# Two banded-mixing layers: the band product with the right projection stationary, in blocks of 128 rows by 128 columns

## The chip, the core and the metric

The kernel runs on one core of a Trainium2 chip, as one launch, in 32-bit floating point throughout. The metric is the device time of that launch in microseconds (us). The kernel before takes 4958.63 us, the median of three runs (4953.22 to 4959.0).

Five engines of the core work side by side, each through its own instructions in order: TensorE (PE; its weight loads are shown apart as PEld), VectorE (DVE), ScalarE (ACT), GpSimd (POOL), and SyncE (SP), which here only issues DMAs. Matrix products land in PSUM, eight banks of 512 floats per partition; everything else is held in SBUF, 128 partitions wide. A matrix product keeps one operand in the array (the stationary operand, put there by a weight load) and streams the other past it (the moving operand).

## The reference

The input `x` is 512 by 512 positions with 64 channels. Two layers are applied, each as `x = x + conv(group_norm(x))`. Cut to what matters, a layer is:

```python
xn = layer_norm(group_norm(x))                 # group norm: 32 groups of 2 channels, over all positions
left  = (xn @ Wl) * mask * sigmoid(xn @ Wlg)   # 64 -> 128 channels
right = (xn @ Wr) * mask * sigmoid(xn @ Wrg)
gate  = sigmoid(xn @ Wog)
# band: for every output row i, offsets d in -4..4
out[i, j, h] = sum_d left[i + d, i, h] * right[i + d, j, h]
out = layer_norm(out) * gate                   # over the 128 channels
y = out @ Wo                                   # 128 -> 64 channels, then x + y
```

Only nine entries per column of `left` are needed, those within four rows of the diagonal. For each hidden channel `h` the band is a matrix product over rows: a banded matrix made of `left`, times `right`. The second layer's group norm needs the channel sums and the channel square sums of the first layer's whole result, so the second layer begins only when the first has ended.

## The kernel before

**Blocks and chunks.** A row block is 64 rows, and consecutive blocks overlap by 8 rows, so a block gives 56 result rows (60 at the two edges); nine blocks cover 512 rows (`row_blocks`, line 67). The 128 partitions hold the same 64 rows twice, once for column `j` and once for column `j + 256`. A chunk is one row block by 128 such column pairs, so a layer has 18 chunks. A chunk has 16 units of 8 column pairs. A layer's loop (`layer`, line 704) runs over steps `t`, one input unit per step, and everything else is hung on that count.

**What a step does.** The order within a step is written out by hand (lines 765 to 847), and every call goes through a wrapper (lines 365 to 378) that keeps each engine's queue in that order:

- `load` (390) fetches a unit of `x`; `affine` (426) applies the group norm, two POOL operations per unit; `inner_stats` and `inner_norm` (431, 435) are the layer norm, four DVE statistics and two POOL operations.
- `transposed` and `kept` (441, 460) turn the unit by TensorE and copy it to `zT` with ScalarE; `kept` also stores it to a DRAM buffer `later`.
- `right` (487), twice per step: four products with a 64x128 piece of `zT` stationary, a sigmoid on ScalarE, and a DVE product into the big SBUF tile `RO`.
- `left` (497) runs five times at the start of a layer (steps 3, 5, 7, 9, 11). It computes the entries near the diagonal and writes them by small DMAs into a DRAM buffer `left_of`, which was filled with zeros first. `take_left` (527) reads it back as the banded matrix `A`.
- `mix` (539) is the band product, for 8 channels at a time, 16 calls per chunk. `A` (64 x 64, columns 16 floats apart in memory) is stationary and `RO` (64 x 128) moves; the two partition halves work in opposite corners of the array. The result goes back over `RO`, half by ScalarE and half by DVE.
- `out_stats` and `solve` (571, 577) give the mean and the inverse deviation of the result; `solve` runs every fourth step, some four operations on DVE and some twelve on POOL, for the input and the output norm together.
- `norm` (610): eight ScalarE operations per output unit. `recall` and `gates` (618, 622): the unit's `zT` is read back from `later`, and its gate is computed by two products of 448 moving columns per unit. `turned` (641): sixteen transposes, then two DVE operations that multiply by the gate into `ZH`. `end` (673): sixteen products with `Wo`, added to the residual `XR`, which POOL has biased (`biased`, 667), and stored.
- `sums` (692), in the first layer only: eight products per unit gather the channel sums and square sums in one PSUM bank. For the sums, a column of ones stands on either side of each piece of `XR`, so its rows are 130 floats long.

An output unit trails its input unit by 30 steps (`LAG`, line 707).

**Buffers.** PSUM holds two double banks (`ps2`, for `right`, `transposed` and `mix`), three single banks in the first layer and four in the second, and one bank for `sums`.

**Start.** 300 us go by with the group statistics of `x`, the weights, and the zero fill of `left_of`. The scratch pool of the set-up is freed then, and the tiles that take its place (`RO`, `XR`, `ZH`) wait for the zero fill that reads it.

## Time and profile before

| what | value |
|---|---|
| median of three runs | 4958.63 us |
| span of the profiled execution | 4957.7 us |
| PE busy | 4186.4 us (84%) |
| DVE, ACT, POOL busy | 3836.3, 3645.2, 3826.5 us |
| DMA engines' mean busy share, steady part | 0.72 |
| mean granted TensorE clock | 0.940 |

The profile lists, for each engine, how long its instructions were busy, and groups equal instructions with their count, busy time and mean duration in ns. Three further views are used below: busy time by stretches of the span, the waits (who waited for whom, in total, times, and the longest), and the timeline (instructions in order of time, equal neighbours merged). A `DMA_DIRECT2D` on `SPq` is the issue of a DMA on SyncE's queue, not its transfer. Nearly all code stands under L373, the wrapper's line, so groups are told apart by tile names.

The first output of layer one is biased at 529.9 us and the last at 2622.7 us; in layer two these are 2888.6 and 4949.1 us. In between, a chunk takes 119 us.

### The profile page before, as it was taken

The numbers are of one execution on the slowest core, as the hardware profiler recorded it, in microseconds if no ns is written. First come the engines' busy times: TensorE is split into PE (matmuls) and PEld (weight loads), VectorE is DVE, ScalarE is ACT, GpSimd is POOL, SyncE is SP. The second block draws the span as 40 slices with busy tenths as digits, with TensorE's granted clock in tenths as the row PEclk, the third lists the DMA queues.
The fourth block names the chain that finished last, engine by engine and source line by source line (L and its number), as shares of the span: only waits on it lengthen the run. The fifth ranks groups of instructions, "written<-read, shape, count | busy, mean of one in ns | idle before, by whom it ended". The sixth has DMA issues, their size and how long they took to land. (4 is left out here: it accounts for less than half of the span.)

```text
span 4957.7 us, 173298 instructions
## 1 busy us (share of the span) xinstructions
PE 4186.4 (84%) x67090; PEld 3543.6 (71%) x67090; DVE 3836.3 (77%) x9635; ACT 3645.2 (74%) x8156; POOL 3826.5 (77%) x4739
## 2 busy tenths in 40 slices
PE   1036899999999999999974689999999999999998
PEld 0025788888888888888763577777777777777775
DVE  6855788888888888888766578888888888888876
ACT  0013788888888888888872378888888888888888
POOL 0037888888888888888534788888888998889853
PEclk6558999999999999999996899999999999999999
DMA  7844677777777777777653467777777777777765
GB/s 305 338 156 130 182 203 207 204 207 204 204 203 204 205 206 206 202 207 210 187 143 88 129 181 205 202 207 205 203 206 202 205 206 205 208 207 209 209 184 152
DMA packets 905343, 982.32 MB, mean 198 GB/s; under 512 B 114210, under 2 KB 641608, under 8 KB 900168
## 3 DMA queue, kind: packets, MB, share of 16 engines
q1 hardware_dynamic: 899840, 969.73, 66.9%
q8 instruction: 531, 8.70, 0.8%
q14 instruction: 292, 2.39, 0.2%
q10 hardware_dynamic: 4680, 1.50, 0.1%
HBM read 658.42 MB, written 312.46 MB: 196 GB/s over the span
## 5 line engine op out<-in xcount | busy, mean ns | idle before, releaser
L373 ACT ACTIVATE on<-RO,nm,rs 128x128 f32<-128x128 f32 x4608 | 1872.5, 496 | 130.1 <-POOL nm L373 110.3
L373 PE MATMUL banks<-pack,zT 64*128 64x256 f32 x9360 | 1325.0, 405 | 148.6 <-DVE RO L373 67.8
L373 PEld LDWEIGHTS banks<-pack,zT 64*128 64x128 f32 x9360 | 886.7, 194 | 517.6 <-DVE RO L373 220.1
L373 PE MATMUL banks<-RO,A 64*64 64x128 f32 x18432 | 1154.3, 277 | 12.7 <-ACT zT L373 12.7
L373 DVE TENSOR_TENSOR RO<-banks,sg 128x512 f32<-128x512 f32 x1152 | 789.9, 686 | 421.1 <-ACT sg L373 402.9
L373 PEld LDWEIGHTS banks<-RO,A 64*64 64x64 f32 x18432 | 1082.3, 183 | 38.6 <-ACT zT L373 15.2
L373 ACT ACTIVATE sg<-banks 128x512 f32<-128x512 f32 (+1 forms) x1188 | 695.0, 587 | 372.5 <-PE banks L373 288.6
L373 DVE BATCH_NORM_STATS2 sto<-RO 128x6 f32<-128x256 f32 x2304 | 842.8, 413 | 1.2
L373 DVE SCALAR_TENSOR_TENSOR ZH<-bank,pack,gate 128x448 f32<-128x448 f32 (+1 forms) x1152 | 738.4, 683 | 71.5 <-ACT gate L373 46.9
L373 DVE COPY RO<-banks 128x512 f32<-128x512 f32 x576 | 396.3, 691 | 487.6 <-ACT RO L373 487.0
L373 POOL TENSOR_TENSOR z<-z,gb 128x512 f32<-128x512 f32 x536 | 687.1, 1282 | 42.0
L373 PE MATMUL bank<-pack,ZH 128*64 128x64 f32 x18432 | 682.8, 229 | 6.1 <-ACT gate L373 5.6
L373 POOL TENSOR_TENSOR z<-z,ga 128x512 f32<-128x512 f32 x536 | 687.8, 1283 | 0.1
L373 POOL TENSOR_TENSOR z<-z,rs 128x512 f32<-128x512 f32 x586 | 618.0, 1055 | 46.0
L373 PEld LDWEIGHTS bank<-pack,ZH 128*64 128x64 f32 x18432 | 602.1, 141 | 48.2 <-ACT gate L373 9.6
L373 POOL TENSOR_TENSOR z<-z,sti 128x512 f32<-128x512 f32 x586 | 627.2, 1070 | 0.0
L373 ACT ACTIVATE gate<-bank 128x448 f32<-128x448 f32 (+1 forms) x1152 | 565.9, 543 | 81.1 <-PE bank L373 66.9
L373 PEld LDWEIGHTS bank<-ident,on 64*128 64x128 f32 x9216 | 409.7, 140 | 260.5 <-ACT gate L373 145.3
L373 PE MATMUL bank<-ident,on 64*128 64x64 f32 x9216 | 450.2, 227 | 137.9 <-ACT gate L373 107.3
L373 PE MATMUL bank<-zg,pack 64*128 64x448 f32 (+1 forms) x2304 | 559.5, 558 | 2.2 <-DMA zg<-later 1.5
L373 POOL TENSOR_TENSOR XR<-XR,pack 120x512 f32<-120x512 f32 (+1 forms) x352 | 418.4, 1190 | 160.6 <-DMA XR<-in_x_dram 58.9
L373 ACT COPY RO<-banks 128x512 f32<-128x512 f32 x576 | 333.5, 583 | 234.1 <-PE banks L373 234.0
(145 smaller groups left out, 3683.3 us busy)
## 6 DMA issues: line engine op xcount, KB each, us to landing
later<-zT SPq DMA_DIRECT2D x576, 256.0 KB
A<-left_of SPq DMA_DIRECT2D x576, 256.0 KB
zg<-later SPq DMA_DIRECT2D x576, 256.0 KB
z<-in_x_dram SPq DMA_DIRECT2D x576, 128.0 KB
z<-mid_x SPq DMA_DIRECT2D x576, 128.0 KB
gn_x<-in_x_dram SPq DMA_DIRECT2D x16, 4096.0 KB
XR<-in_x_dram SPq DMA_DIRECT2D x448, 112.0 KB
mid_x<-XR SPq DMA_DIRECT2D x448, 112.0 KB
```

Of the source, the lines that this page charges most:

```text
L373: return lambda *a, **k: tc.keep_in_program_order(f(*a, **k))
```

## The change

A block is now 128 rows, with 120 new rows per block, and a chunk is 128 rows by 128 columns; the last 32 rows of all four column quarters together form one tail chunk. A layer has 4 x 4 + 1 = 17 chunks of 16 input units.

In `mix`, a 64 x 128 piece of `RO` is stationary (columns 2 floats apart) and 64 or 68 columns of `A` move. The result has the 128 columns `j` on the partitions and the rows `i` along the free axis. The halves overlap by 8 rows, which are added by a DVE operation of their own. Each of the 512 x 512 output positions is then normed, gated and projected once: an output unit is 8 rows (or 4, `ni = 1`) by 128 columns, and there are 260 per layer, 8 of them of 4 rows.

Moved and altered with it:

- Input units are 32 rows by 4 x 8 columns, loaded by one DMA. `zT` is a tile of four units. `right` runs four steps later (`LATE`) and takes as stationary operand the same column of all four units, 16 floats apart.
- `later` is laid out by chunk. `recall` reads four runs of 512 bytes per partition where one of 2 KB was read. `gates` becomes eight products of 128 columns.
- `turned` writes its transposes into PSUM with the innermost step 64 floats.
- `left` writes into a free part of `RO` and sends runs of nine floats to DRAM.
- `XR` is contiguous, one DMA each way. The mask is a scalar per partition, so `solve` uses one small operation per column quarter.
- `sums` keeps the square sums; the channel sums come from the accumulating output of the DVE operation in `turned`, added up per chunk.
- The `XR` and `ZH` clearing, the `fewer` constant and its DMAs go.

The core of the diff:

```diff
-JW = 16
+JW = 24
+LATE = 4
+STEP = P - 2 * WIN
+AW = S + 3 * WIN
-HA = 16
-NA = 3
+HA = 8
+NA = 4
@@ load
-            for e, j in enumerate((u.j, LH + u.j)):
-                en.sync.dma_start(u.z[e * S : (e + 1) * S], src[rows, j : j + JU, :])
+            en.sync.dma_start(
+                u.z.rearrange("p j c -> p (j c)"),
+                strided(
+                    src, (i * L + j + 32 * u.s) * D, (L * D, 32), (JU * D, 4), (1, JU * D)
+                ),
+            )
@@ right
+        t = zT[u.n].rearrange("c r (i k g) -> c k g (r i)", k=4, g=4)
+        pr = projected(lambda part, k: t[part, k, u.g], q, w["right"])
@@ left
+                    en.sync.dma_start(
+                        strided(
+                            left_of, ((row + r) * H + t) * AW + a + r,
+                            (R4 * H * AW + R4, nq), (2 * AW, H // 2), (1, NEAR),
+                        ),
+                        side[q0 : q0 + nq, :, t, NEAR * r : NEAR * (r + 1)],
+                    )
@@ mix
-                        ph[part, hh, :], lhsT=A[part, :, h0 % HA + hh],
-                        rhs=R[part, (h0 + hh) // 2, :, hh % 2],
+                        o, lhsT=RO[part, (h1 + h) // 2, c.place : c.place + JC, h % 2], rhs=rhs,
...
+            en.scalar.copy(o[:, :, :m0], x)
+            en.vector.tensor_copy(o[:, :, m0:], y[:, :, v:])
+            if v:
+                o = o[:, :, m0 - v : m0]
+                todo.append((o, o, y[:, :, :v], ALU.add))
@@ norm
-        for j in range(JU):
+        for j in range(R4 * o.ni):
@@ recall
-        en.sync.dma_start(o.t, later[o.at])
+        o.t = t[:, : 256 * o.ni].rearrange("c (s x) -> c s x", s=SUB)
+        en.sync.dma_start(o.t, later[o.chunk.c][:, :, o.i4 * S : (o.i4 + o.ni) * S])
@@ gates
+        for k in range(4):
+            for e, pg in enumerate(pgs):
+                en.tensor.matmul(
+                    pg.rearrange("h (k y s g) -> h k s y g", k=4, s=SUB, g=4)[:, k],
+                    lhsT=w["gate"][part],
+                    rhs=o.t[part].rearrange("c s (y k g) -> c k s y g", k=4, g=4)[:, k],
@@ turned
+                v = pt.rearrange("h (r y s) -> h y s r", r=JU, s=JU)
+                en.tensor.transpose(v[:, i], o.on[part, i, :], ident[part, part])
...
+            more = {"accum_out": acc_to(n)} if acc_to else {}
@@ start
-        z = left_of.rearrange("b (p n) -> (b p) n", n=S * (S + 2 * WIN) // 2)
-        for n in range(0, z.shape[0], P):
-            en.sync.dma_start(z[n : n + P], nothing[: min(P, z.shape[0] - n)])
+        for b in range(n_blocks):
+            for i in range(2):
+                en.sync.dma_start(
+                    left_of[b][:, i * H * AW // 2 : (i + 1) * H * AW // 2], nothing
+                )
```

## Prediction

> **What bounds the kernel now.** I read the busy time by stretches first, one stretch in the steady part of each layer.

> ```profile
> core 0: us, PE busy (x) PEld busy (x) DVE busy (x) ACT busy (x) POOL busy (x), PEclk, DMA share, GB/s
> 900.00:1500.00 600.00, 574.85 (x9991) 502.67 (x9992) 487.70 (x1226) 504.06 (x1127) 534.46 (x642) 0.99 0.72 205
> 3000.00:3600.00 600.00, 551.38 (x8681) 466.47 (x8679) 492.25 (x1224) 502.75 (x1122) 532.92 (x645) 0.98 0.72 204
> ```

> TensorE is busy 96% and 92% of the time, GpSimd 89% in both. A chunk takes 119.3 us in layer one and 118.8 in layer two, although layer two lacks `sums`. What two stretches with different TensorE work and one pace share is GpSimd: 534.5 and 532.9 us. So I ask what it waits for (waits in 3000 to 4200 us; columns: total, times, longest).

> ```profile
> DVE RO L373 <- ACT RO L373: 112.6, 130, 2.0
> PEld banks L373 <- DVE RO L373: 80.6, 140, 1.7
> POOL rsqrt L373 <- DVE rs L373: 61.3, 40, 3.6
> PEld banks L373 <- POOL z L373: 36.7, 36, 1.1
> POOL XR L373 <- DMA XR<-mid_x: 4.4, 6, 1.5
> ```

> GpSimd waits almost only at `solve`, 61 us in 1200 or 6.1 us per chunk. With 106 busy (533 / 600 x 119) that leaves 7 us per chunk, some 80 ns ahead of each instruction, which I count as issue. GpSimd thus has 6 us per chunk to give, and TensorE 5 in layer one and 10 in layer two. Both are near the pace.

> The groups of instructions by shape (count, busy us, mean ns) give the prices:

> ```profile
> L373 PEld LDWEIGHTS banks<-RO,A 64*64 64x64 f32 x18432 | 1082.3, 183 | 38.6 <-ACT zT L373 15.2
> L373 PEld LDWEIGHTS bank<-pack,ZH 128*64 128x64 f32 x18432 | 602.1, 141 | 48.2 <-ACT gate L373 9.6 <-DVE ZH L373 0.6
> L373 PEld LDWEIGHTS bank<-zg,pack 64*128 64x128 f32 x2304 | 225.2, 190 | 34.3 <-DVE ZH L373 3.3 <-DVE RO L373 1.7
> L373 POOL TENSOR_TENSOR XR<-XR,pack 120x512 f32<-120x512 f32 x224 | 266.8, 1191 | 7.1 <-DMA XR<-mid_x 5.7 <-DVE sto L373 1.0 <-DVE RO L373 0.4
> ```

> A weight load of 64 contiguous columns has 141 ns, one of 128 has 190, and the 64 columns of `A`, 16 floats apart, have 183: a wide step makes the load slower. The timeline of one step gives rates:

> ```profile
> 1203.52 0.92 PE L373 MATMUL bank<-zg,pack 64*128 64x448 f32 x4
> 1204.27 1.03 PE L373 MATMUL banks<-pack,zT 64*128 64x256 f32 x8
> 1205.13 0.69 PE L373 MATMUL bank<-ident,on 64*128 64x64 f32 x16
> 1207.65 3.94 PE L373 MATMUL banks<-RO,A 64*64 64x128 f32 x64
> ```

> From start to the next group's start, `gates` takes 0.75 us and `turned` 0.58 (62 ns per pair of halves). Two `mix` calls run to 1211.52 us, 3.87 us or 121 ns per pair. Each fp32 product is two such instructions.

> [...]

> **The change part by part.** Sums are against the profiled span, 4957.7 us, 1 us under the median.

> *Chunks.* 17 for 18: one chunk less per layer, -119 us each, if the pace holds.

> *GpSimd.* Units keep their four operations. Per chunk of 15 output units one `XR` operation goes, -1.2 us, and the mask's small operations add about 1. It stays at 113 us plus up to 6 of waiting.

> *Mix on TensorE.* As many instructions per chunk; 64 columns move instead of 128, but 128 are loaded instead of 64. Loads run under the products before them[...]. I take no change; nothing is won here.

> *Gates.* 8 pairs of 128 columns, taken at the present `mix` rate less its slack, 115 ns: 0.92 us for 0.75. Per chunk 15 x 0.92 - 16 x 0.75 = +1.8.

> *Right.* Its loads step 64 bytes[...]: +2.4 per chunk.

> *Turned.* Sixteen transposes per unit[...]. Below: free [...]; above: doubled, 62 to 124 ns per pair, 0.5 us per unit. I take half, 0.25 x 15 = +3.8 per chunk.

> *One output unit less per chunk* on TensorE: 0.58 + 0.98 (`end`) + 0.57 (`sums`) = -2.1, in layer two -1.6.

> *TensorE's sum per chunk.* Layer one 574.85 / 5.03 = 114.3 + 1.8 + 2.4 + 3.8 - 2.1 = 120.2; with 3 of its 5 us of idle time, 123. Layer two 109.6 + 6.4 = 116; with 2 idle, 118. So TensorE sets the pace in layer one, and stands level with GpSimd (113 to 119) in layer two. Against 119: 16 x 4 - 119 = -55, and 16 x -1 - 119 = -135.

> *DVE and ScalarE.* ScalarE's norms fall from 4608 to 4096, one unit's eight or 3 us per chunk. DVE: the copy in `mix` is an eighth shorter and a small add follows (about 0.2 us), `ZH` is 512 wide instead of 448, and layer one adds two accumulator reads per unit (0.06 to 0.16 us each, its shortest clearing and its shortest tensor operation here). Saved statistics balance it. DVE has 21 us per chunk free; were that gone, the add would cost 3 us per chunk. The four 124-row chunks of a layer split each `mix` in two: within the idle I kept.

> *DMA.* `XR` moves in runs of 2 KB instead of 512 bytes, `zg` the other way; `A` grows from 256 KB x 2 to 304 KB x 2 per 16 channels. The share stays near 0.72. SyncE issues about 6 instead of 10 per step. Hidden; without cover a late `A` would stop TensorE.

> *Left.* 96 DMAs per layer instead of 108, but up to 1024 runs of 36 bytes where there were 128 of 64 to 256. SyncE's timeline, and all DMA in 0.3 us around the first of the 8 KB transfers:

> ```profile
> 352.65 12.65 SPq L373 DMA_DIRECT2D left_of<-sg x27
> ...
> DMA packets 144, 0.01 MB, mean 28 GB/s; under 512 B 144, under 2 KB 144, under 8 KB 144
> ```

> The 144 fall into 28 of that view's 40 slices, 0.21 us or 1.5 ns each. The new DMAs have 853 runs on average: 1.3 us each (estimate), 125 us for 96, where issue alone now takes 12.65 / 27 = 0.47 each, some 50 us. From step 3 to step 16, where `A` is wanted behind them, it is then 125 + 35 for SyncE's other DMAs = 160, for 115 now (324 to 439 us): +45. Then 17 steps to the first output, for 14 now, at 6 us: +18. On the other side `sg` no longer waits for these DMAs (67 us now, both layers), and `zT` has eight steps for its stores. I take +45 per layer, between -25 (issue binds) and +190 (twice the price). Queued behind them on SyncE: `z` loads, seven steps ahead, then `A`, then all of `mix`.

> *Start.* The zero fill grows from 21.2 to 24.9 MB, +10 us at the 385 GB/s that the stretch 240 to 280 us shows. But GpSimd and DVE no longer stand 47 us before `XR` and `ZH` clearing that waits for it; their first units run under it, some -20. Together -10. Channel sums at the layer's end: about nil.

> *Sum.* -55 - 135 + 90 - 10 = -110: a span of 4848, rounded to 4845 as a median.

> **Rivals.**

> - *The waits go and `left` hides.* With TensorE at 119 and 113 per chunk and no longer fill: -119 - 215 - 10, about 4615. For it: ScalarE and SyncE are relieved. Against: TensorE's sums.
> - *The scattered transposes double.* TensorE 124 and 120, pace 127 and 122: +9 - 71 + 90 - 10 = +18, 4975. [...]
> - *Slower: the stationary side costs by its step.* Place: `mix`, 256 pairs per chunk. [...] It decides from about 135 ns per pair: each ns costs 256 x 16 x 2 = 8.2 us, and 110 / 8.2 = 13. For it: `A`'s 183 ns. Against: [...] loads for two halves side by side in `right` today.
> - *Slower: the small runs cost double.* 2.6 us per DMA: +125 per layer, 5095. [...] Against: today's 64-byte runs are cheap.
> - *The change does not do what it says:* 17 chunks and 4096 norms follow from the diff, so only their worth is open.

> **How the numbers follow.** Forecast 0.45 (own range 4740 to 4940), faster still 0.08, doubled transposes 0.20, stationary loads 0.12, small runs 0.12, rest 0.03. 0.2% is 10 us, about what a measurement of this kernel can tell from no change. Faster: 0.42 + 0.08 + 0.05 of the doubled case and rest = 0.55; same 0.05; slower 0.40. The range 4700 to 5110 leaves out the stationary loads and most of the fastest case.

> **What would show it.** Chunks 123 and 118 us apart in the `XR` operations of GpSimd; `mix` at 115 to 125 ns per pair; `turned` 0.6 to 1.1 us; first output of layer one near 560 us. It is wrong if `mix` gets cheaper (then GpSimd alone sets 113 to 119), if loads of `RO` show over 200 ns, or if the `left` DMAs end after 520 us in layer one.

## The result, and the profile after

| | before | after |
|---|---|---|
| median | 4957.11 us (4 runs, 4953.22 to 4959.0) | 5757.2 us (4 runs, 5751.47 to 5773.5) |
| ratio, 95% interval | | 1.1616 [1.1596, 1.1637] |
| span of the profiled execution | 4957.7 us | 5759.5 us |
| first `XR` bias operation on GpSimd, layer one | 529.9 us | 667.2 us |
| from there to the layer's last one | 2092.7 us | 2343.6 us |
| from there to layer two's first | 265.9 us | 418.0 us |
| from there to layer two's last | 2060.5 us | 2321.4 us |

The change is 16% slower where 2% faster was forecast, outside the range too. The four lower rows, read from the two traces, split the 802 us between their spans: 137 and 152 in the fill of the two layers (the time before a layer's first output), 251 and 261 in their steady parts, although a chunk less is worked off in each.

Busy time by stretches, steady part of each layer:

```profile
core 0: us, PE busy (x) PEld busy (x) DVE busy (x) ACT busy (x) POOL busy (x), PEclk, DMA share, GB/s
1500.00:2100.00 600.00, 532.82 (x8938) 506.33 (x8932) 412.82 (x1185) 414.90 (x909) 437.80 (x535) 0.93 0.63 180
4200.00:4800.00 600.00, 515.25 (x7988) 483.42 (x7986) 422.26 (x1083) 424.12 (x935) 460.35 (x557) 0.92 0.65 185
```

Nothing is full any more. In layer one TensorE falls from 96% to 89%, GpSimd from 89% to 73%, and the TensorE clock from 0.99 to 0.93. An engine that is busy for less of a longer time is not the bound; something makes them all wait. The waits in 4200 to 5400 us of the kernel after:

```profile
DVE RO L394 <- ACT sg L394: 238.8, 175, 3.5
ACT sg L394 <- PE banks L394: 189.6, 126, 3.8
PE banks L394 <- DVE RO L394: 145.3, 117, 3.6
POOL XR L394 <- DMA XR<-mid_x: 100.3, 24, 7.4
```

Read from the third line: TensorE waits 117 times for a VectorE copy into `RO`, and from that ScalarE waits for TensorE's projections, and VectorE for ScalarE's sigmoids. The groups by shape show no price that rose enough to explain it (the first line is of the kernel before):

```profile
L373 PEld LDWEIGHTS banks<-pack,zT 64*128 64x128 f32 x9360 | 886.7, 194 | 517.6 <-DVE RO L373 220.1
L394 PEld LDWEIGHTS banks<-pack,zT 64*128 64x128 f32 x8704 | 1164.8, 308 | 729.0 <-DVE RO L394 306.2
L394 PEld LDWEIGHTS banks<-A,RO 64*128 64x128 f32 x17408 | 1109.9, 201 | 104.1 <-ACT RO L394 42.3 <-issue 22.8 <-ACT zT L394 17.1
L394 POOL TENSOR_TENSOR XR<-XR,pack 128x512 f32<-128x512 f32 x504 | 550.0, 1092 | 630.6 <-DMA XR<-mid_x 317.0 <-DMA XR<-in_x_dram 255.5 <-PE bank L394 41.2
L394 DVE DVE_READ_ACCUMULATOR ZH<-bank,pack,gate 128x1 f32 x520 | 43.1, 83 | 0.0
```

The loads of `right`, whose columns now lie 64 bytes apart, went from 194 to 308 ns. Most of that is hidden under the products: in the kernel with both edits of the mixes (below), the two `right` calls of a step take 2.03 us to the next group's start where they took 1.83 before, 3.2 us per chunk. The accumulating output shows as a second instruction (`DVE_READ_ACCUMULATOR`) of 83 ns, where the prediction had 60 to 160.

Then the timeline of one step with two `mix` calls (start, duration, engine, and in brackets the idle time before):

```profile
1500.41 3.98 PE L394 MATMUL banks<-A,RO 64*128 64x64 f32 x64
...
1500.94 3.21 ACT L394 ACTIVATE on<-RO,nm,rs 128x128 f32<-128x128 f32 x8 [1.37 <-DVE ZH L394]
...
1504.06 1.04 ACT L394 COPY RO<-banks 128x512 f32<-128x512 f32 x2
...
1504.65 1.16 DVE L394 COPY RO<-banks 128x448 f32<-128x448 f32 x2 [2.36 <-ACT RO L394]
...
1505.73 0.34 DVE L394 TENSOR_TENSOR RO<-RO,banks 128x64 f32<-128x64 f32 x2
...
1506.08 2.02 PE L394 MATMUL banks<-pack,zT 64*128 64x256 f32 x8 [1.69 <-DVE RO L394]
```

Here the loss can be seen whole. The first call is through at 1502.5 us, but its pair of banks is free only at 1505.9: ScalarE is at its eight norms until 1504.1, VectorE waits for ScalarE's copy, and the overlap add of the first call comes after the copies of both (the loop over `both`, lines 941 to 945). Both double pairs are then held, the next `right` finds none, and TensorE stands for 1.69 us. The `right` that follows takes 2.02 us, where the same eight instructions took 1.03 to 1.13 before: it runs at half clock, which the trace shows granted from 1506.40 to 1509.82 us. In the kernel before, the same step had just enough room: VectorE's copy of the first call ended at 1211.33 us, 0.2 us before the second call was through, and `right` followed without a gap:

```profile
1210.65 0.68 DVE L373 COPY RO<-banks 128x512 f32<-128x512 f32 x1
...
1211.52 1.14 PE L373 MATMUL banks<-pack,zT 64*128 64x256 f32 x8
```

From the start of one `end` on TensorE to the next (layer one), a step without `mix` takes 5.7 us in both kernels, and one with a single `mix` 7.2. A step with two took 9.0 us and now takes 10.9 to 13.5, 12.4 most often. Six steps of a chunk are such. From the first output of a chunk to that of the next it is some 140 us in layer one and 133 to 143 in layer two, and 151 to 165 us for the first four chunks of a layer. Those have an output unit more, and beside the outputs of the first three run the split `mix` calls of the next 124-row chunk.

The fill is the other part. SyncE's timeline and all DMA from 330 to 500 us:

```profile
323.25 38.67 SPq L394 DMA_DIRECT2D left_of<-RO  x24
...
DMA packets 75946, 5.82 MB, mean 34 GB/s; under 512 B 74407, under 2 KB 74407, under 8 KB 75943
```

The issue of one DMA takes 1.6 us of SyncE where it took 0.47 before. Packets of under 512 bytes, nearly all of 36, fill the 16 engines, for 34 GB/s. In the trace the 81,920 runs of 36 bytes of layer one's `left` took 38.4 ns on average: 81,920 x 38.4 / 16 = 197 us, and SyncE issues them from 323 to 507 us.

### The profile page after: what moved, and what is told of

It is laid out like the page before. It is cut to its first block, busy times and chain, and to the rows that moved or that the text cites. A ratio compares the mean times of both kernels' runs of the same rounds, so it can differ in the third digit from the quotient of the medians.

```text
span 5759.5 us, 170176 instructions
## 1 busy us (share of the span) xinstructions
PE 4420.8 (77%) x67808; PEld 4116.1 (71%) x67808; DVE 3666.9 (64%) x10114; ACT 3371.1 (59%) x7514; POOL 3536.8 (61%) x4475
## 5 line engine op out<-in xcount | busy, mean ns | idle before, releaser
L394 DVE TENSOR_TENSOR RO<-banks,sg 128x512 f32<-128x512 f32 (+1 forms) x1124 | 764.0, 685 | 1029.0 <-ACT sg L394 1001.6
L394 ACT ACTIVATE sg<-banks 128x512 f32<-128x512 f32 x1106 | 656.6, 594 | 1080.8 <-PE banks L394 1064.3
L394 PE MATMUL banks<-A,RO 64*128 64x64 f32 (+2 forms) x17408 | 1163.9, 289 | 74.4 <-ACT RO L394 38.9
L394 PEld LDWEIGHTS banks<-A,RO 64*128 64x128 f32 x17408 | 1109.9, 201 | 104.1 <-ACT RO L394 42.3
L394 POOL TENSOR_TENSOR XR<-XR,pack 128x512 f32<-128x512 f32 (+1 forms) x520 | 567.4, 1091 | 634.0 <-DMA XR<-mid_x 318.9
L394 DVE SCALAR_TENSOR_TENSOR ZH<-bank,pack,gate 128x512 f32<-128x512 f32 (+1 forms) x1040 | 723.3, 735 | 74.4 <-ACT gate L394 45.8
L394 PEld LDWEIGHTS bank<-zg,pack 64*128 64x128 f32 x8320 | 711.3, 233 | 28.5 <-issue 4.2
L394 DVE COPY RO<-banks 128x448 f32<-128x448 f32 (+1 forms) x672 | 355.6, 533 | 568.9 <-ACT RO L394 568.1
L394 PE MATMUL bank<-zg,pack 64*128 64x128 f32 (+1 forms) x8320 | 705.0, 317 | 4.6 <-DMA zg<-later 3.0
L394 ACT ACTIVATE gate<-bank 128x512 f32<-128x512 f32 (+1 forms) x1040 | 553.5, 584 | 216.2 <-PE bank L394 198.9
```

What stands on the lines that cost most here:

```text
L394: return lambda *a, **k: tc.keep_in_program_order(f(*a, **k))
```

## The experiments

**The held banks.** Theory 1: the deferred add, and the norms ahead of the first copy, hold the first pair of banks past the end of the second `mix`. Theory 2: GpSimd waits for late `XR` transfers (100 us in 1200), and through it everything else. One edit puts the add behind its own copy:

```diff
-            if n < HB:
+            if todo:
                 en.vector.tensor_tensor(*todo.pop())
```

> Only the place of the overlap add changes: it follows its own copy instead of both mixes. Theory 1 (held bank): the first pair of banks of a double mix is released only after the second mix has been copied too, TensorE stands some 1.7 us before the next right, and the clock falls for the next 3 us; a double-mix step takes 12.4 us instead of the 9.0 of the kernel before. The add is 0.34 us of the hold and the second copy 0.6, so about 0.6 of the 1.7 us should go: six double steps per chunk, 34 chunks, 0.6 us each is 120 us, about 5635, and up to 5400 if the clock then stays up. Theory 2 (late XR): GpSimd waits 108 us in 1200 for XR transfers, which this edit doesn't touch: 5740 to 5770.

Measured: 5465.0 us, ratio to before 1.103 [1.1011, 1.1048]; 292 us won, twice and more what the 0.6 us per step came to. Two of three double-mix steps fell to 9.0 to 10.6 us: where the norms were not late, the first pair was now free before the second call ended.

The second edit spreads the eight norms over the copies of a step, an equal share ahead of each:

```diff
-            if t + 1 in outs:
-                norm(outs[t + 1])
...
+            before_copy()
             en.scalar.copy(o[:, :, :m0], x)
```

> Only ScalarE's order changes: the eight norms of the next output are spread ahead of the copies of the mixes instead of all ahead of the first copy. Theory 1: the first copy can start some 1.6 us earlier, but the add that frees the first pair of banks still stands behind the second copy, so only about 0.3 us of the 1.7 us is won per double step: 5690 (5600 to 5750). If instead ScalarE's late first copy alone were the cause, this edit alone should bring a double step to 9 us: about 5100. Theory 2: 5740 to 5770.

Measured: 5671.9 us, 1.1455 [1.1438, 1.1473]; 85 us won, as theory 1 had it: an early copy helps little while the add stands behind the other one.

> Both edits: add at once and norms spread. Theory 1: the first pair of banks is free before the second mix ends, TensorE no longer stands, the clock stays near 0.98, and a double-mix step falls from 12.4 to about 9.0 us: six steps, 34 chunks, 3.4 us is 690 us: about 5070, with chunks of 123 us. Theory 2 (late XR transfers hold GpSimd, and so the norms): still over 5600.

Measured: 5345.6 us, 1.0792 [1.0776, 1.0808]; 412 us won, more than the two alone (377). The same stretch of a double-mix step:

```profile
1503.41 3.98 PE L394 MATMUL banks<-A,RO 64*128 64x64 f32 x64
...
1506.17 0.62 DVE L394 COPY RO<-banks 128x448 f32<-128x448 f32 x1 [2.26 <-ACT RO L394]
1506.72 0.21 DVE L394 TENSOR_TENSOR RO<-RO,banks 128x64 f32<-128x64 f32 x1
...
1507.23 1.21 PE L394 MATMUL banks<-pack,zT 64*128 64x256 f32 x8
```

The first pair is free at 1506.9, the second call ends at 1507.2, `right` follows without a gap, and the step takes 9.2 us. Theory 2 falls as the main cause. But 5070 was expected: in layer one most chunks stand at 128 us instead of 123, and the three beside split mixes at 144 to 146.

**The small runs.** The rows of `left_of` are laid out as [group of eight channels][column][channel], so that a band run is 9 x 8 floats in a piece; `mix` then reads its moving columns 32 bytes apart.

```diff
-        A = lp.tile([P, HA, AW], F32, tag="A", name="A")
+        A = lp.tile([P, AW, HA], F32, tag="A", name="A")
...
-                            (R4 * H * AW + R4, nq), (2 * AW, H // 2), (1, NEAR),
+                        (R4 * H * AW + R4 * HA, nq), (AW * HA, H // HA), (1, NEAR * HA),
```

> The change with its left rows laid out as [eight channels' group][column][channel], so that a band run is 288 contiguous bytes on both sides instead of 36: 48 DMAs of up to 256 runs per layer for 96 of up to 1024; mix then reads its moving columns 32 bytes apart. Theory 4 (small runs set the fill): 36-byte runs take 40 ns each, 76,800 of them some 190 us of all engines; with wide runs left ends about 130 us earlier in each layer: first GpSimd XR operation near 535 instead of 667 us, about 5500 in all if the step of the moving columns costs nothing. Rival: moving columns 32 bytes apart cost as the strided loads of A did (183 for 141 ns): the 64 instructions of a double mix go from 4.0 to 5.2 us, 10 mixes of 0.6 us per chunk, 34 chunks: 200 us given back, about 5700. Rival: the fill is set by the number of DMAs issued or by something else: first XR operation at 600 us or later.

Measured: 5524.95 us, 1.1146 [1.1116, 1.1176]. The first `XR` operation comes at 529.5 us, before's 529.9; the way between the layers takes 284.7 us for 418.0. The two fills fell by 138 and 133 us, as expected. The edit makes the runs eight times as long, and so an eighth as many, and halves the number of DMAs. At the 0.5 us that one issue now takes, 48 DMAs fewer are worth some 25 us (estimate from 6.33 / 12), so most of it is the small runs. Where 24 DMAs took 38.7 us of SyncE's timeline, 12 now take 6.3:

```profile
321.73 6.33 SPq L394 DMA_DIRECT2D left_of<-RO  x12
```

10,240 runs of 288 bytes took 28.5 ns on average. The moving step did not cost 1.2 us per double `mix`: in the repaired kernels below a double-mix step takes 9.3 us with it and 9.2 without. Only 232 us of the 270 reached the total; the steady parts took 35 us longer, in a kernel whose double-mix steps still hang on the held banks; why they did is not shown.

**The list of GpSimd's work.** What keeps a chunk of the kernel with both edits at 128 us? Its first two mix steps take 10.8 and 11.5 us. The timeline of one of them:

```profile
1739.70 0.20 DVE L394 TENSOR_SCALAR rs<-var 128x64 int32<-128x64 int32 x1
...
1744.39 0.30 POOL L394 TENSOR_TENSOR rsqrt<-rs 128x64 f32<-128x64 f32 x1
...
1749.15 3.19 ACT L394 ACTIVATE on<-RO,nm,rs 128x128 f32<-128x128 f32 x8 [3.94 <-POOL nm L394]
```

VectorE hands `solve` over at 1739.9, GpSimd comes to it at 1744.4, still at units' affines and norms, and the norm that needs it starts 9 us after VectorE was done. `count` (line 833) says how many units GpSimd works ahead in each of the 16 steps of a chunk: in the kernel before, 13 in the ten steps with mixes and three in the six without, which are mostly steps of only 5.7 us. After the change it is 11 and five. The change puts the mixes four steps later (`LATE`) and leaves `count` where it was.

```diff
-        done = -4 - NU
+        done = -5 - NU
...
-            for _ in range(1 if 0 <= t < NU else count[t % NU]):
+            for _ in range(1 if 0 <= t < NU else count[(t - LATE) % NU]):
```

> The kernel with both edits of the mixes (5346), and the list that spreads GpSimd's work ahead over the 16 steps of a chunk moved by the four steps by which the change moved the mixes. Theory 5 (planner out of phase): in the kernel of both edits a chunk takes 128 us in its 120-row form, and its first two mix steps take 10.8 and 11.5 us where 9.2 and 7.2 would do, because GpSimd still has units from the short steps before to work off when the norm needs its solve (ScalarE waits 3.9 us for it). With the list moved these 6 us per chunk go: 34 chunks, about 5140. Rival (the rest is the DMA, or the split mixes): 5300 to 5350.

Measured: 5278.6 us, 1.0657 [1.0631, 1.0682]. The first two mix steps now take 9.3 and 7.3 us and most chunks 121 to 127 and 117 to 122 us in the two layers, so the cause is right; but only 67 us of 200 came. The six beside split mixes stayed at 144 to 151, and the two fills grew by 45 and 42 us (first `XR` operation at 685.1 for 639.9 us; 431.9 for 389.7 between the layers). The list orders the units of a fill too; why moving it lengthens the fill is not shown.

> The same with the left rows laid out for runs of 288 bytes. The fills fell by 137 and 133 us when that was done alone, and nothing in the steady part answers to them: about 250 less than the run with the list moved, so 4890 if that one comes to 5140, under the kernel before. If the list brings nothing, 5090.

Measured: 5009.1 us, 1.01 [1.008, 1.012]: 269 less than the run with the list moved, as the fills promised. Between the two traces, 280 us apart, the fills shrink by 145 and 141 us (first `XR` operation at 540.4 us, 291 us between the layers).

**The split mixes.** In a 124-row chunk 8 x 68 floats don't fit a bank (544, for 512), so each call is made in two, each half in a double pair. The second half is given two single banks:

```diff
-            pb = two_banks()
+            if h1 == h0:
+                pb = two_banks()
+                pb = [pb[:, e * 512 : (e + 1) * 512] for e in range(2)]
+            else:
+                pb = [one_bank() for e in range(2)]
```

> The kernel with all repairs (5009), and in the four 124-row chunks of a layer, which split each mix in two, the second half takes two single banks instead of the second pair. Theory 3 (split mixes): there a chunk takes 147 us in layer one and 150 in layer two, where 122 and 119 plus one more output unit of 7.5 would do; a half mix waits for the pair that the half before it holds, and the next right finds none free. With four sets of banks most of the 17 to 23 us per chunk go: eight chunks, some 110 to 150 us: 4860 to 4900, faster than the kernel before. Rival: the split chunks are slow for their greater number of copies or for late XR transfers: 4990 to 5010.

Measured: 4873.0 us (5 runs), ratio to before 0.9819 [0.9793, 0.9845]. This kernel beats both, the kernel before by about 2%. The three chunks beside split mixes went from 144-147 us to 129-132 in layer one, and from 150 to 122-124 in layer two. Its steady parts:

```profile
core 0: us, PE busy (x) PEld busy (x) DVE busy (x) ACT busy (x) POOL busy (x), PEclk, DMA share, GB/s
900.00:1500.00 600.00, 569.85 (x10126) 547.08 (x10125) 470.81 (x1372) 475.97 (x1042) 503.30 (x613) 0.98 0.73 205
3000.00:3600.00 600.00, 559.94 (x9179) 534.49 (x9180) 475.67 (x1283) 486.20 (x1094) 508.24 (x622) 0.96 0.74 208
```

TensorE is at 95% and 93% again, the chunks after the fourth at 122 to 126 and 118 to 124 us.

**The hold alone, in the kernel before.** Its copy by VectorE is split (112 and 16 of 128 columns) and the second piece is made after both mixes, as the add is in the change:

```diff
-                en.vector.tensor_copy(o, v)
+                en.vector.tensor_copy(o[:, :, :c1], v[:, :, :c1])
+                late.append((o[:, :, c1:], v[:, :, c1:]))
...
+            for args in both:
+                en.vector.tensor_copy(*args)
```

> The kernel before, in which VectorE's copy of a mix leaves the last 16 of its 128 columns to a second copy, and that second copy is made after both mixes of a step, as the change makes its overlap add. Theory 1: the first pair of banks is then held till about 1.6 us after the second mix, TensorE stands, the clock falls, and double-mix steps go from 9.0 to about 12.4 us: six per chunk, 36 chunks, up to 730 us, so 5400 to 5680. Rival (the hold matters only with the change's other costs): under 5100.

> Control for the held kernel: the same split copy, the second part right after the first. Only one short VectorE copy of some 0.2 us more per mix, ten per chunk, in VectorE's idle time: 4945 to 4990. If the extra instruction itself were what costs, this one is as slow as the held one.

Measured: held 5229.9 us, 1.0553 [1.0537, 1.0568]; the control, 4967.7, 1.0022 [1.0013, 1.0031]. So the hold is a cause by itself, 262 us over the control, and the extra instruction is not; but it is well short of the 440 to 720 us expected. The step went to 10.5 us and not to 12.4:

```profile
1007.26 0.89 DVE L373 COPY RO<-banks 128x448 f32<-128x448 f32 x3 [1.17 <-ACT RO L373]
1008.16 1.14 PE L373 MATMUL banks<-pack,zT 64*128 64x256 f32 x8 [1.57 <-DVE RO L373]
```

TensorE stands 1.57 us and then `right` runs in 1.14 us, at full clock. The fall of the clock needs something that the kernel before hasn't got.

**What lets the clock fall.** Theory 6: the short moving side. Each product of `mix` in the kernel before is cut in two of 64 columns:

```diff
-                    en.tensor.matmul(
+                    for p in (slice(0, S), slice(S, JC)):
+                        en.tensor.matmul(
-                        ph[part, hh, :], lhsT=A[part, :, h0 % HA + hh],
-                        rhs=R[part, (h0 + hh) // 2, :, hh % 2],
+                            ph[part, hh, p], lhsT=A[part, :, h0 % HA + hh],
+                            rhs=R[part, (h0 + hh) // 2, p, hh % 2],
```

> The kernel before with each product of the mixes cut in two of 64 moving columns, each with its own weight load, so the same arithmetic in twice the instructions, without any held bank. Theory 6 (the short moving side lets the TensorE clock fall): among the rights that follow a double mix, none of 186 took over 1.6 us in the kernel before; here some tens of per cent should take about 2 us, and the granted clock of the steady part fall from 0.99 to about 0.95. Rival (only idle TensorE lets it fall): no right over 1.6 us, clock 0.98 or more. The time grows in either case, by up to 3.5 us per double mix and 1.8 per single one [...].

Measured: 5854.3 us (one run). A double-mix step takes 12.4 us: a pair of half the columns takes 114 ns where one of 128 took 121, and there are twice as many. The clock of 900 to 1500 us is 0.99, and none of the 148 `right` calls after a double mix (900 to 4800 us) took over 1.6 us; the 257 named in the next expectation took in calls after single mixes. Theory 6 falls as put. Then both together, short products and the held banks:

> The kernel before with both: products of 64 moving columns and the held bank. Neither alone let the clock fall (no right over 1.6 us among 257 and 174). Theory 6b (a gap of some 1.6 us beside a mix of short products is what lets it fall): some of the rights after a double mix take about 2 us here. Rival (neither; the changed kernel's 128 weight columns or another wait in the step matter): again none. The time should stand some 1.5 us per double step, 36 chunks of six, 300 us, over the unheld one of 5854 at an unchanged clock.

Measured: 6400.2 us (one run), 546 more. One such step:

```profile
1012.08 0.89 DVE L373 COPY RO<-banks 128x448 f32<-128x448 f32 x3 [2.93 <-ACT RO L373]
1012.98 2.00 PE L373 MATMUL banks<-pack,zT 64*128 64x256 f32 x8 [1.55 <-DVE RO L373]
```

The same gap of 1.55 us, and now `right` takes 2.00. `right` calls after a double mix that took over 1.6 us (trace, 900 to 4800 us), where a gap of over 0.1 us stood before them: before 0 of 56, held 0 of 168, held with short products 54 of 132, after 46 of 112. In the kernel before, it takes both. In the changed kernel a gap just before `right` is not the whole account: all 31 calls without one were slow too.

## Why the prediction was wrong, point by point

- *The pace: TensorE's sum, 123 and 118 us per chunk.* The repaired kernel comes near it (123.2 and 120.9 on average over ten of the 120-row chunks), and 17 chunks, the DMA share (0.73) and GpSimd as the next engine hold. Part of that is luck: TensorE is busy for 117 and 113.5 us of a chunk, where 120 and 116 were summed up, and idle for 6 and 7, where 3 and 2 were. In the change as made it is 140 and more, because TensorE's work is not what sets the end of a double-mix step.
- *"DVE has 21 us per chunk free."* This step failed first. I priced the copy and the add by their busy time, against a free share, and asked what each costs and not when the pair of banks is free. The second loop was in the diff; the question of who waits for the first pair was not put to it. The cost: 292 us for the add alone, 412 with the norms ahead of the first copy.
- *The four 124-row chunks "within the idle I kept".* 136 us for both layers. The price of a split call lies in the buffers it takes, not in its instructions.
- *`left` at 1.3 us per DMA, +45 per layer.* The mechanism, runs before issue, was right; the size was off. The trace of after gives 853 x 38.4 / 16 = 2.0 us, and the fills +137 and +152. My 1.5 ns per run came from runs of 64 bytes, in a stretch where the engines were 27% busy. The rival of small runs put 2.6 us per DMA and 125 per layer on top of the 45; the runs came out between the two.
- *`count`* has no line in my working. I counted the later steps for the start and did not ask what else is hung on the step number: 67 us in its place, measured on top of the first repair, and in a run whose fills came out 87 us longer; in the steady parts of both layers 161 us were won (4143.5 for 4304.2).
- *The clock*, 0.99 then and 0.93 now, is not in the working either. Between the first and the last output of a layer TensorE was granted half clock for 120 us before, 890 after and 247 in the repaired kernel, both layers together. I had no ground for it: once per chunk of layer two, a gap of 1.5 us stood before `right` in the kernel before, at full clock. That 64 columns move in place of 128 is in the working, but not what it does to the clock.
- *`mix` on TensorE.* Right: 3.98 us for 64 instructions by the records, and in the kernel of both edits 3.82 us from its start to that of `right`, 119 ns per pair, where 115 to 125 were named. That a pair would take no longer with 128 columns loaded was my estimate; no trace of before showed it. The slower rival by stationary step falls, although these loads show 201 ns, over the 200 that I had named as a sign.
- *`right`.* +2.4 us per chunk was predicted and some 3.2 came. The price behind it was my estimate; no trace of before showed loads of 128 columns that lie 64 bytes apart. They take 304 ns in the repaired kernel, where the contiguous ones took 194.
- *`gates` and `turned`.* 0.89 us for 0.92 predicted; and sixteen scattered transposes take 491 ns at the least and 496 in the median to the start of the next group (layer one, 900 to 2400 us), where the contiguous ones took 490 and 609. Half a doubling was predicted, so the 3.8 us per chunk were not there, nor was the rival that doubled them. Both were my estimates: the kernel before has no scattered transposes to read a price from.
- *Two readings.* GpSimd's 7 us per chunk are 55 ns ahead of each of some 128 instructions, and not 80. The 0.58 us of `turned` are 73 ns per pair of halves; 62 is what the next step's 0.50 us give. Neither moves the sum.
- *The sum.* 5757 less the four repairs (412, 67, 269, 136) is 4873, 28 us above the forecast. That they meet so closely is luck in part: in the traces the steady parts of the repaired kernel win 124 us over the kernel before, where 190 were forecast, and its fills cost 37, where 80 were (90 for `left` less 10 for the start). What was costed at nothing, too low or not at all made 884 us, against the 90 set down for `left`.

## What to carry to other kernels

For every buffer that a change touches, write down when it is taken and when it is freed, and who takes it next: here an instruction of 0.2 us in idle time held a bank for 2 us longer (1006.1 to 1008.0 us in the held kernel above). When a change moves a loop's phase, look for every list that is indexed by the same step number. Count DMA runs with a price from runs of the same size (9.0 ns for 64 bytes before, 38.4 for 36 after). And when products get shorter, count the columns moved per microsecond: here a double `mix` came to 3,660 per 3.413 us, for 7,200 before, and the clock fell 160 times between 900 and 4800 us, for 31.

## What the runs showed that I had not expected

- The TensorE clock: with gaps of some 1.6 us after products of 128 moving columns no `right` ran slow (0 of 168 calls), nor did one after products of 64 columns without held banks (0 of 148); with both together 54 of 132 did. What sorts these cases, and also the 14 of 168 slow `right` calls that stood without a gap in the repaired kernel, is the sum of columns moved in 3.41 us: all 62 of that kernel's falls between 900 and 4800 us follow pieces under 3,050. Why the columns sort the cases better than the busy time is open.
  Within such a piece TensorE need not be idle: in the trace of after, the 160 pieces ahead of a fall (900 to 4800 us) moved 2,240 columns in the median. Of all 231 times at half clock there, 144 lasted 3.41 us. The same eight instructions took 2.00 us at half clock (short products, held banks) and 1.14 at full (held banks alone).
- Runs of 36 bytes to DRAM took 38.4 ns on average, at a DMA share of 90% or more in most slices of 330 to 500 us, those of 64 bytes 9.0 ns, of 256 bytes 22 and of 288 bytes 28.5. The average hides two kinds: 90% of the 36-byte runs took 12 ns or less, and the 9% that took over 50 ns hold three quarters of the time. What holds those up, and whether the size or the odd start matters, was not tried.
- Transposes that write neighbouring elements 256 bytes apart in PSUM took no longer than contiguous ones (223 ns for 222 in the median of one, 491 for 490 at the least in sixteen).
